# One twelve-bit product for gate and up in a pre-norm attention and quantised feed-forward kernel

## The chip, the cores and the metric

The kernel runs on one core of a Trainium2 chip. Its time is the device time of one execution in microseconds (us), the median over several runs. TensorE is written PE here, VectorE DVE, ScalarE ACT, GpSimd POOL; SP is the engine whose queue issues most transfers.

## The reference

One transformer layer on x of shape (2, 1024, 512): layer norm, attention with 32 heads of 16, residual; layer norm, a feed-forward part with quantised numbers, residual.

```python
x = x + attn(_layernorm(x), w_q, w_k, w_v, w_o)          # softmax(q k^T / 4) v, then w_o
x = x + ffn(_layernorm(x), w_gate, w_up, w_down, ...)

def int4_quant(x):                                        # integers -8..7 times a scale per token
    beta = jnp.mean(jnp.abs(x), axis=-1, keepdims=True)
    x_q = jnp.clip(jnp.round(x * SQRT7 / (beta + EPS)), -8, 7)
    return x_q * (beta * SQRT7) / SQRT7

def bitlinear(x, w, scale):                               # weights -1, 0, 1 times one mean
    w_mean = jnp.mean(jnp.abs(w))
    w_q = jnp.clip(jnp.round(w / (w_mean + EPS)), -1.0, 1.0)
    return jnp.einsum('...i,oi->...o', x, w_q * w_mean * scale)

xq = int4_quant(x)
gate = jnp.square(jax.nn.relu(bitlinear(xq, w_gate, s_gate)))   # w_gate, w_up: (1376, 512)
inter = int8_quant(bitlinear(xq, w_up, s_up) * gate)
return bitlinear(inter, w_down, s_down)                         # w_down: (512, 1376)
```

Inputs of gate and up are small integers and their weights are -1, 0 or 1, so their products are integers.

## The kernel before

**Attention.** The main loop goes through 32 steps, one for each batch, half of the queries (512), group of 128 features and half s of its heads (four heads at a time). A step has eight slots, one for each 128 keys. In each slot `scores` is called twice. It runs the row maxima of one step (`max_mm`, L475, reduced on DVE at L485) beside the exponentials of the step before (`exp_mm`, L515, ACT at L519). Both use fp32r matmuls on 32 rows of the array, and they share three pairs of PSUM banks in turn. Between the two calls `weigh_values` (L545) multiplies the exponentials of an earlier slot with V. After the last slot of two steps `normalise` divides by the sums, which go out to DRAM and back to be spread over rows; `normalise_last` does this on chip for the last pair, in four column blocks.

**Fillers.** Everything else is a generator that yields after each piece of work. The class `Fillers` keeps four lists (`proj`, `norm`, `ffn`, `back`) and steps them between the score calls, in the order of their due slots. A slot's second `fill.run` has a budget in nominal nanoseconds of PE, SHARE = 1300, or MORE = 1800 while a projection is due within 16 slots; pieces name their price in `yield ("pe", 900.0)`. A first `fill.run(100.0, short=True)` admits only short pieces. A piece that needs PSUM takes the spare bank (`ps_o`, one buffer) and gives it back for the next `run`; inside the loop no other bank is to be had. `_back` steps the `back` list and begins the first tasks of the `proj` and `norm` lists, so that their weights are fetched. `ensure` runs `fill.run(1e9)` until the named projections are done, just before a step's loads on SP (`load_k`, `load_q`, `load_v`). After the loop `fill.turn` steps every ready task once per round, and the score banks are spare too.

**Projections.** `project_qk` (L351) and `project_v` (L418) use plain fp32 matmuls. Q and K are split into a high and a low part: ACT copies PSUM to `full`, POOL makes `hi` and `lo`, SP stores both. `project_v` fetches its weights (L333) for each half of the tokens. The four `w` buffers are shared by all projections.

**Feed-forward.** `weight_sums` reads the three weight matrices once in pieces of 512 columns or less to get the means. `weight_quant` reads them again; POOL compares with the lower threshold (L677), DVE with the upper and subtracts (L679), and the results are kept in fp8. For each of 16 tiles of 128 tokens `output_proj` (L714) adds the residual and computes the statistics, `ffn_input` quantises and transposes, `ffn_product` (L801) multiplies, and `ffn_output` quantises `inter` (L841 to L853), transposes it and multiplies with `wd` (L880). The product takes the 1376 columns in chunks of 512, 512 and 352:

```python
for f, j in ((gate, 0), (gate, 1), (up, 0), (gate, 2), (up, 1), (up, 2)):
    yield from f(j)
```

`gate` is four matmuls, a Relu on ACT (L811) and a square (POOL L815, or ACT L813 for the last four tiles); `up` is four matmuls and one DVE multiply from PSUM (L823). The last four tiles can only start after the last step, so they run after the loop.

## Time and profile before

| | |
|---|---|
| median of 3 runs | 1307.87 us (1304.2 to 1317.62) |
| profiled execution: time, span | 1320.16 us, 1318.4 us |
| PE, DVE, ACT, POOL busy | 92%, 66%, 54%, 19% of the span |
| mean granted PE clock | 0.965 of full |
| PE idle, 66 to 264 us | 23.8 of 198 us |
| PE busy, 264 to 1188 us | 97 to 99% in the stretches of 132 or 66 us, except 264 to 396 and 924 to 1056 (96%) |
| last pso matmul ends | 1221.5 us |

Spans on PE are modelled: a matmul's record goes past the start of the next one, so the distance between starts tells more than a duration. In a line of the timeline the columns are start, duration, engine, line, operation, tiles and shapes; a bracket names the idle time before it and what ended it. In a line of groups, the number behind `x` is a count, then busy us and mean ns, then idle time of the engine and its releasers. A plain fp32 matmul is recorded as two.

### The profile page before, as it was taken

How to read it: one execution, taken by the hardware profiler on the slowest of the kernel's cores; microseconds unless marked ns; L12 is line 12 of the kernel's file. 1: busy time of each engine (PE TensorE's matmuls, PEld its weight loads, DVE VectorE, ACT ScalarE, POOL GpSimd, SP SyncE). 2: the span in 40 equal slices, each digit the busy share in tenths (PEclk: the TensorE clock that was granted, in tenths of full speed). 3: DMA queues.
4: the chain of work that ended last, by engine and by line, in shares of the span. 5: the costliest groups of instructions: out<-in, count | busy, mean ns of one | idle time of the engine just before them, and what ended most of it. 6: DMA issues, size and time to landing. Idle time of an engine off the chain costs nothing.

```text
span 1318.4 us, 22143 instructions
## 1 busy us (share of the span) xinstructions
PE 1209.3 (92%) x9082; PEld 541.6 (41%) x9082; DVE 866.5 (66%) x1203; ACT 712.1 (54%) x903; POOL 246.5 (19%) x279
## 2 busy tenths in 40 slices
PE   5768899999999999999999999999999999999566
PEld 2345444334445443444444444444433344443222
DVE  6521468778865667687776676877776867772634
ACT  1124655545655555665666556666665556666243
POOL 1034326455511100321101003110010111100000
PEclk9889999999999999999999999999999979999769
DMA  3056666555333431221213223211133110201000
GB/s 112 0 184 216 225 199 214 156 177 191 126 107 122 136 110 58 89 81 58 72 47 106 95 76 117 76 55 67 57 107 95 58 57 34 82 26 33 24 0 33
DMA packets 72334, 127.88 MB, mean 97 GB/s; under 512 B 9680, under 2 KB 30160, under 8 KB 72232
## 3 DMA queue, kind: packets, MB, share of 16 engines
q1 hardware_dynamic: 64360, 101.16, 23.8%
q0 software_dynamic: 7872, 25.30, 5.9%
q8 instruction: 71, 1.16, 0.4%
q14 instruction: 31, 0.25, 0.1%
HBM read 89.25 MB, written 37.19 MB: 96 GB/s over the span
## 4 chain that ended last, share of the span: by engine, by line
PE 74%; DVE 11%; ACT 5%; issue 4%; DMA 4%; POOL 2%; SPq 0%; ACTq 0%; DVEq 0%; POOLq 0%
PE pse L515 22%; PE pso L545 16%; PE psm L475 8%; PE psy L714 5%; PE psv L418 4%; DVE pm L485 4%; PE psq L351 3%; PE pu L801 3%; PE py L880 3%; PE psk L351 3%; DMA wv<-in_wvT 2%; PE pg L801 2%; ACT e L519 2%; PE psn L498 1%; PE psk L390 1%
## 5 line engine op out<-in xcount | busy, mean ns | idle before, releaser
L485 DVE TENSOR_REDUCE pm<-psm 128x2 f32<-128x1024 f32 x512 | 621.5, 1220 | 336.9 <-PE pse L515 236.8
L519 ACT ACTIVATE e<-pse 128x1024 f32<-128x1024 f32 x512 | 523.0, 1024 | 415.3 <-PE pse L515 315.4
L475 PE MATMUL psm<-kst,qst 32*128 32x512 f32 x2048 | 372.8, 448 | 13.4 <-ACT e L519 8.2
L515 PE MATMUL pse<-qst,kst 32*128 32x512 f32 x2048 | 371.7, 446 | 10.2 <-DVE pm L485 8.8
L515 PEld LDWEIGHTS pse<-qst,kst 32*128 32x128 f32 x2048 | 151.5, 185 | 325.0 <-issue 160.6
L545 PE MATMUL pso<-e,v 128*32 128x512 f32 x2048 | 277.5, 612 | 0.7 <-ACT po L554 0.4
L515 PE MATMUL pse<-mrow,onesr 2*128 2x512 f32 x1024 | 208.6, 406 | 0.0
L475 PEld LDWEIGHTS psm<-kst,qst 32*128 32x128 f32 x2048 | 152.5, 186 | 39.1 <-ACT e L519 27.9
L515 PEld LDWEIGHTS pse<-mrow,onesr 2*128 2x128 f32 x1024 | 95.3, 185 | 5.1 <-ACT mrow L502 0.2
L815 POOL TENSOR_TENSOR g<-g 128x512 f32<-128x512 f32 (+1 forms) x36 | 34.2, 951 | 315.6 <-ACT g L811 315.6
L418 PE MATMUL psv<-wv,xnT 128*128 128x128 f32 x512 | 70.7, 294 | 14.2 <-DMA wv<-in_wvT 12.0
L545 PEld LDWEIGHTS pso<-e,v 128*32 128x32 f32 x2048 | 40.7, 108 | 97.4 <-issue 94.5
L418 PEld LDWEIGHTS psv<-wv,xnT 128*128 128x128 f32 x512 | 64.0, 203 | 27.3 <-issue 19.7
L714 PE MATMUL psy<-wo,OT 128*128 128x512 f32 x128 | 66.7, 635 | 5.9 <-DVE OT L597 5.9
L351 PE MATMUL psq<-xnT,wq 128*128 128x512 f32 x120 | 60.9, 622 | 1.4 <-ACT full_k L359 1.4
L351 PE MATMUL psk<-xnT,wk 128*128 128x512 f32 x112 | 58.4, 640 | 1.5 <-ACT vst L430 1.5
L677 POOL TENSOR_SCALAR low<-raws,whalf 128x512 bf16<-128x512 f32 (+2 forms) x35 | 52.8, 1510 | 21.4 <-DMA raws<-in_wuT 8.5
L801 PEld LDWEIGHTS <-xqT 128*128 128x128 bf16 x384 | 33.1, 102 | 57.5 <-issue 38.0
L770 POOL TENSOR_SCALAR xn<-x,mv,a 128x512 f32<-128x512 f32 x12 | 24.9, 2073 | 166.8 <-DVE a L747 166.7
L801 PE MATMUL pg<-wg,xqT 128*128 128x512 fp8e4 (+1 forms) x192 | 49.9, 387 | 4.0 <-DVE inter L823 2.4
L801 PE MATMUL pu<-wu,xqT 128*128 128x512 fp8e4 (+1 forms) x192 | 47.6, 372 | 3.5 <-ACT g L811 2.5
L880 PE MATMUL py<-wd,iqT 128*128 128x512 fp8e4 (+1 forms) x176 | 45.1, 392 | 2.9 <-ACT g L811 1.7
(124 smaller groups left out, 841.6 us busy)
## 6 DMA issues: line engine op xcount, KB each, us to landing
v<-vD SPq DMA_DIRECT2D x32, 512.0 KB
kst<-kD SPq DMA_DIRECT2D x30, 512.0 KB
qst<-qD SPq DMA_DIRECT2D x60, 256.0 KB
vD<-vst POOLq DMA_DIRECT2D x32, 256.0 KB, 5.4
qD<-hi_q SPq DMA_DIRECT2D x30, 256.0 KB
qD<-lo_q SPq DMA_DIRECT2D x30, 256.0 KB
x<-in_x SPq DMA_DIRECT2D x16, 256.0 KB
wq<-in_wqT SPq DMA_DIRECT2D x16, 256.0 KB
```

The costliest lines, as they stand in the source:

```text
L351: nc.tensor.matmul(ps, w[:, c, :], xnT[b, h][:, c, :], start=(c == 0), stop=(c == KC - 1))
L418: nc.tensor.matmul(ps[:, i * P : (i + 1) * P], xnT[b, half][:, c, i * P : (i + 1) * P], w[:, c, :], start=(c == 0), stop=(c == KC - 1),)
L475: nc.tensor.matmul(ps[:, r % 2, :], qst[n][l][rows, t * P : (t + 1) * P], kst[n][rows, kh * QB : (kh + 1) * QB], start=(l == 0), stop=(l = ...
L485: nc.vector.tensor_reduce(pm[n][:, t, kh, 2 * j : 2 * j + 2], ps, AX.X, ALU.max, negate=True)
L515: nc.tensor.matmul(ps[:, r % 2, :], left, right, start=(l == 0), stop=(l == 2))
L519: nc.scalar.activation(e, ps, AF.Exp, scale=SCALE)
L545: nc.tensor.matmul(acc[n][32 * r : 32 * r + 32, :], vt[n][:, i, r, :], e[r // 2][:, r % 2, :], start=(i == 0), stop=(i == NT - 1),)
L677: nc.gpsimd.tensor_scalar(low, w, h[:rows, m, 1:2], None, ALU.is_lt)
L714: nc.tensor.matmul(ps, OT[b, h, g][:, i * P : (i + 1) * P], wo[g], start=(g == 0), stop=(g == NG - 1),)
L801: nc.tensor.matmul(ps, xT[:, c, :], w[:, c, n : n + size], start=(c == 0), stop=(c == KC - 1))
L815: nc.gpsimd.tensor_tensor(g2[j], g2[j], g2[j], ALU.mult)
L880: nc.tensor.matmul(py, iqT[:rows, c, :], wd[:rows, c, :], start=(c == 0), stop=(c == FC - 1))
```

## The change

Gate and up weights are kept in one fp32r matrix, `wgu = 3400 * up + gate`, each entry an integer of at most twelve bits. One product gives 3400 * U + G in PSUM. ACT divides by 3400 and rounds by adding and subtracting 1.5 * 2^23 (two passes), which gives U; DVE takes 3400 U away from PSUM, which leaves G. Relu, square and multiply then follow on POOL; for the last four tiles DVE does Relu and square in one step. The transposed inputs `xqT` become fp32r too.

```diff
+PACK = 3400.0
@@ ensure
-        while not set(names) <= self.done:
-            self.run(1e9)
+        tasks = [t for t in self.tasks["proj"] if t["name"] in names]
+        due = max((t["due"] for t in tasks), default=0)
+        while not set(names) <= self.done:
+            self._back()
+            task = 1
+            while task:
+                task = next(
+                    (t for t in self._candidates() if (t["due"] <= due and t["list"] == "proj" or t["kind"]) and self._ready(t)),
+                    None,
+                )
+                if task:
+                    self._step(task)
+            self.now += 1
@@ norm_inputs
-            nc.sync.dma_start(xs[t], x[b, t * P : (t + 1) * P, :])
+            (nc.scalar if fast and t % 2 else nc.sync).dma_start(xs[t], x[b, t * P : (t + 1) * P, :])
...
+            if fast and half == 0 and i % 2:
+                nc.vector.tensor_copy(dst, ps.rearrange("p (c t) -> p c t", c=KC))
+            else:
+                nc.scalar.copy(dst, ps.rearrange("p (c t) -> p c t", c=KC))
@@ project_qk
-        full = sb.tile([P, QB], F32, tag="full", name=f"full_{name}", bufs=1)
-        nc.scalar.copy(full, ps)
-        nc.gpsimd.tensor_copy(hi, full)
-        nc.gpsimd.tensor_tensor(lo, full, hi.bitcast(F32), ALU.subtract)
+        lo = sb.tile([P, QB], F32, tag="lo", name=f"lo_{name}", bufs=2)
+        nc.scalar.copy(lo, ps)
+        nc.gpsimd.tensor_copy(hi, lo)
+        nc.gpsimd.tensor_tensor(lo, lo, hi.bitcast(F32), ALU.subtract)
@@ project_v
-        w = proj_weights(wvT, g, f"wv_{b}_{g}_{half}")
-        yield ("gap", 4)
+        if half:
+            w = wt.pop((b, g, "v"))
+        else:
+            w = wt[b, g, "v"] = proj_weights(wvT, g, f"wv_{b}_{g}")
+            yield ("gap", 4)
@@ normalise_last (now a task of the back list)
+        OT[b, h, g] = ot
         for i in range(TQ):
+            if i == 2:
+                yield from done([f"out_{b}_{h}_0"])
...
+            fill.done.add(f"tokens_{i}")
+            yield ("gap", 1)
@@ load_raw, weight_sums: whole rows of 1376 columns (two of 512 for wd), two buffers
-        t = sb.tile([P, 512], F32, tag="raw", name=f"{name}{m}_{c}_{n}", bufs=4)
-        nc.gpsimd.dma_start(t[:rows, :cols], ap[c * P : c * P + rows, n : n + cols])
+        t = sb.tile([P, I], F32, tag="inter", name=f"{name}{m}_{c}", bufs=2)
...
+            nc.gpsimd.dma_start(part, ap[(c + i) * P : (c + i) * P + rows, :])
@@ weight_quant: order up, gate, down
+                low = below(m, c, part)
+                yield ("gap", 2)
...
+                    w = wgu[:, c, :]
+                    if m == 1:
+                        above(w, m, part, low, ALU.subtract)
+                    else:
+                        nc.vector.scalar_tensor_tensor(w, w.bitcast(F32), PACK, low, ALU.mult, ALU.subtract)
+                        yield ("gap", 1)
+                        above(w, m, part, w.bitcast(F32), ALU.add)
@@ output_proj
+                if last and g == NG - 1:
+                    yield from done([f"tokens_{i}"])
@@ ffn_input (DVE normalises only the first of the last four tiles, POOL the others)
+        first = last and i == 0
+        (nc.vector if first else nc.gpsimd).tensor_scalar(xn, xt, mean, a, ALU.subtract, ALU.mult)
@@ ffn_product
+            ps = spare(f"pgu_{k}_{n}")[:, :size]
             for c in range(KC):
                 nc.tensor.matmul(
-                    ps, xT[:, c, :], w[:, c, n : n + size], start=(c == 0), stop=(c == KC - 1)
+                    ps, xT[:, c, :], wgu[:, c, n : n + size], start=(c == 0), stop=(c == KC - 1)
                 )
...
+            nc.scalar.activation(up[j], ps, AF.Identity, bias=magic, scale=1.0 / PACK)
+            nc.scalar.activation(up[j], up[j], AF.Identity, bias=negmagic)
+            nc.vector.scalar_tensor_tensor(part, up[j], -PACK, ps, ALU.mult, ALU.add)
             yield ("give",)
             yield ("pe", 900.0)
+            if last:
+                nc.vector.scalar_tensor_tensor(part, part, 0.0, part, ALU.max, ALU.mult)
+            else:
+                nc.gpsimd.tensor_scalar(part, part, 0.0, None, ALU.max)
+                nc.gpsimd.tensor_tensor(part, part, part, ALU.mult)
+            nc.gpsimd.tensor_tensor(part, part, up.pop(j), ALU.mult)
@@ the order of the work
+                ready = ready + [name]
-    SHARE, MORE = 1300.0, 1800.0
+    SHARE, MORE = 1000.0, 1800.0
+        fill.WIDTH["proj"] = 4 if "first_1" in fill.done else 7
```

In `ffn_output` the last four tiles lose two pauses, and `cd` is computed after `inter` is scaled. V's second half now also waits for its first half.

## The prediction

> **What bounds the kernel now.** I read the page's busy shares and clock first, then busy time by stretch, the groups of instructions kept apart by shape, the chain of waits, and last the timeline of one ordinary slot, of the opening and of the end.
>
> ```profile
> PE 1209.3 (92%) x9082; PEld 541.6 (41%) x9082; DVE 866.5 (66%) x1203; ACT 712.1 (54%) x903; POOL 246.5 (19%) x279
> ...
> PEclk9889999999999999999999999999999979999769
> ```
>
> TensorE is the fullest engine. The share hides three stages, which the busy time by stretch shows (length, then PE, PEld, DVE, ACT, POOL busy, clock, DMA):
>
> ```profile
> 66.00:99.00 33.00, 21.00 (x125) 13.86 (x124) 7.07 (x6) 8.82 (x21) 10.99 (x20) 0.90 0.53 184
> 660.00:792.00 132.00, 130.24 (x1038) 58.55 (x1036) 93.11 (x122) 76.18 (x91) 8.48 (x9) 1.00 0.25 81
> 1253.00:1286.00 33.00, 22.77 (x87) 9.00 (x88) 12.42 (x26) 13.86 (x24) 0.00 (x0) 0.69 0.00 0
> ```
>
> From 264 to 1188 us PE is busy 96 to 99% of every stretch and DVE about 72%, so work taken off PE there shortens the run, unless a wait replaces it. Before 264 and after 1188 PE has holes, and chains of waits set the time.
>
> The middle, from the timeline of two slots (start, duration):
>
> ```profile
> 646.69 0.77 PE L801 MATMUL pu<-wu,xqT 128*128 128x352 fp8e4 x4
> 647.39 0.73 PE L515 MATMUL pse<-qst,kst 32*128 32x512 f32 x4
> ...
> 864.33 1.04 PE L801 MATMUL pu<-wu,xqT 128*128 128x512 fp8e4 x4
> 865.30 0.49 PE L515 MATMUL pse<-qst,kst 32*128 32x512 f32 x2
> ```
>
> A group of four product matmuls holds PE for 865.30 - 864.33 = 0.97 us at 512 columns and 647.39 - 646.69 = 0.70 us at 352. Without filler a slot is two score calls of 0.9 us and one pso of 1.0, some 2.85 us, against two 1.22 us reductions on DVE; so PE, not DVE, sets it.
>
> **Middle: product.** Removed: one of two product groups for each of 3 chunks, for 12 of the 16 tiles (the last four run after the loop). Per tile 2 x 0.97 + 0.70 = 2.64 us, times 12 = -31.7 us.
>
> The new product reads fp32r on 128 rows. No row shows that at 512 columns. From below: the fp32r score matmuls on 32 rows start in rounds 0.23 us apart (640.19, 640.42, 640.65 in that timeline), the pace of the fp8 group (0.97 / 4 = 0.24). From above: the four-fold fp32 of L351, 1.91 us for two matmuls, 0.95 each. psn (L498) is fp32r on 128 rows, at 128 columns: four in 0.66 us, each 0.29, so one per (0.66 - 0.29) / 3 = 0.12; four-fold would be 0.95 / 4 = 0.24. It is nearest in shape and not four-fold, so I take 0.24 us for 512 columns. An fp32 weight load lasts 185 to 203 ns against 102 for bf16; the later ones run under matmuls, the first of a chunk doesn't: 36 x 0.09 = +3.2 us.
>
> **Middle: unpacking.** These rows price it:
>
> ```profile
> L811 ACT ACTIVATE g<-pg 128x512 f32<-128x512 f32 x32 | 19.0, 595 | 12.6 <-PE pg L801 12.0 <-DVE d L845 0.6
> L813 ACT ACTIVATE g<-g 128x512 f32<-128x512 f32 x8 | 5.0, 629 | 0.3
> L887 DVE SCALAR_TENSOR_TENSOR y<-py,cd,x 128x512 f32<-128x512 f32 x16 | 11.9, 744 | 11.4 <-PE py L880 11.4
> L815 POOL TENSOR_TENSOR g<-g 128x512 f32<-128x512 f32 x24 | 24.9, 1040 | 224.2 <-ACT g L811 224.2
> ```
>
> A chunk needs ScalarE 0.60 + 0.63 us, then DVE 0.74, then GpSimd. Behind the second ScalarE pass queues the next slot's exponential (1.02 us), and the score call after pso waits for it to free its PSUM pair. Follow a slot from the end of a product, t = 0: the previous exponential ends at 0.2, the two passes at 1.43, the next exponential at 2.45; the second score call starts at 1.9 and wants the pair at 2.14. Stall about 0.35 us per chunk, 36 x 0.35 = +12.6 us. From below nothing is exposed (other filler lies between). From above, the wait seen behind other ScalarE work: 0.65 us of PE at 1179.59, after 1.43 + 0.45 us on ScalarE; with the DVE step behind it, 0.9 each, +32. DVE's queue too stands still until 1.43, then does 0.74 and two reductions, done at 4.7; the call needing the last pair comes near 6, so I price that at nothing; were that slack gone, each chunk would cost up to 0.74.
>
> GpSimd goes from 1.04 to about 1.6 + 1.04 + 1.04 = 3.7 us per chunk (1.6 from the L677 row). It is busy 8.48 of 132 us in the 660 stretch: nothing; without that cover the gm reduction, and the score reductions queued behind it on DVE, would wait 3.7 us.
>
> The budget of filler falls from 1300 to 1000 a slot. By the yields a tile's product falls from 5400 to 2700, the non-short work of a tile from 7900 + 3440 = 11340 to 8640: ratio 0.76 against 0.77. Costed at nothing; a tile left over would pay the tail's pace, 10.9 us.
>
> Middle: -31.7 + 3.2 + 12.6 = **-16** (bounds -32 to +4).
>
> **Weight preparation.** The GpSimd comparison keeps its total (L677, 52.8 us) but comes in pieces of 1606 x 1376 / 512 = 4.3 us; DVE has 12 steps of 2.0 us (L679, 745 ns, scaled) where there were 24 totalling 16.7. Queued behind them are reductions on DVE and the hi/lo splits on GpSimd; behind those the stores and loads on SP. Slots of 4.4 us (266 of them from 27 to 1203 us) leave DVE 2.0, so little shows: **+3** (0 to +8, 12 steps late by 0.7). Fewer, longer GpSimd fetches have one ahead in place of two or three; 5 to 7 us from issue to landing now, 8 us between uses then: nothing.
>
> **Opening.**
>
> ```profile
> 77.83 18.57 DMA wv<-in_wvT
> 96.53 6.65 PE psv L418 x32
> ...
> 135.51 14.31 DMA wv<-in_wvT
> 149.86 3.46 PE psv L418 x16
> ```
>
> These pieces of the chain are V weights arriving late: `ensure` runs any ready filler, so a V projection not yet due is put in PE's queue ahead of the scores and PE stops 8.7 us (and 3.3 at 149.86). The change fetches V weights once per pair and lets `ensure` run only what is due. The matmuls it skips run later, where PE is full: no gain. The 12.0 us of waiting go. Bounds: nothing, if another fetch is late (the held buffer blocks SP's queue: 4.7 us seen behind psv) and all of PE's holes from 66 to 264 us, 12.0 + 3.6 + 4.3 + 0 + 3.9 = 23.8. Splitting x over SP and ScalarE's queue (four issues took 1.81 us; ScalarE is idle until 12.99) is under 1 us, counted at nothing, like the split evacuation and the hi/lo split that now needs no `full` buffer. **-12** (-24 to 0).
>
> **End.** Now all four columns of the last normalisation precede the statistics: xq of the first tile is ready at 1252.0, the last column at 1231.1. After the change tiles 0 and 1 need two columns (1226.9), their last matmul 1.9, add 0.7, statistics 0.9, inverse root 2.5, absolute sums 1.9, factors 1.3, quantising 1.4: 1237.5, 14.4 us earlier. Columns 2 and 3 (4.2 us of DVE) and leftover output work compete: -10 (-14 to -4). The products then:
>
> ```profile
> 1254.78 1.87 PE L801 MATMUL pg<-wg,xqT 128*128 128x512 fp8e4 x4 [0.67 <-ACT xqT L782]
> ...
> 1257.33 1.86 PE L801 MATMUL pg<-wg,xqT 128*128 128x512 fp8e4 x4 [0.68 <-ACT g L811]
> ```
>
> One spare bank makes each chunk wait for its reader. The first tile takes 14.4 us (to 1269.16). With three chunks of 1.87 + 0.60 + 0.63 + 0.74 + 0.1 = 3.95, the last 2.9, and squaring and multiplying (1.4), 12.2. The other three take 10.9 each now; by the same sum 8.3 at full clock, 10.8 at half. I take 2.2 + 3 x 1 = -5 (-10 to 0). The 16 us after the last product stay. **-15** (-24 to -4).
>
> The granted clock from 1252 to 1270 was 0.50 with PE busy 12.1 of 18 us, and 1.00 from 1275. [...]
>
> **Sum.** -16 + 3 - 12 - 15 = -40. The profiled execution took 1320.2 us (span 1318.4, 1.8 around it), 0.9% above the median of 1307.87. 1320.2 - 40 = 1280; the same proportion off the median gives **1268 us**.
>
> **Rivals.** *Freed PE time comes back as idle time.* The chunk's stall is 0.8 us, the middle gains nothing, both ends gain: 1308 + 3 - 27 = 1284. For it: PE already waits at 1179.59; against: only 13.4 us of PE's idle time stands before psm. 0.13. *The ends give nothing*, the late fetch is replaced by another and the final chain by DVE's crowded queue: 1308 - 16 + 3 = 1295. For: SP and DVE keep their order; against: the waits are long and named. 0.07. *Slower: the spare bank.* In the loop filler has one bank, and it stays taken through both ScalarE passes and the DVE step, with an exponential ahead 3.1 us. If the next filler group, or short transposes 1.9 us after, meets it held, PE stops, scores behind it too. At 2 us a chunk: 36 x 2 + 3 - 32 = +43, with the ends -24: 1308 + 19 = 1327. It decides from (31.7 - 3.2 + 24) / 36 = 1.5 us a chunk. For: FIFO queues; against: 2.85 us of scores lie between. 0.09. *No single pass*: fp32r on 128 rows at L351's pace, 3.8 us a chunk for the 1.94 saved, on 48 chunks +90: 1308 + 90 - 24 = 1374. 0.03.
>
> **Numbers.** The forecast has 0.68 and its own range, 1236 to 1290; taking in the first two rivals gives 1236 to 1303. Over 1% is about what a measurement here tells from no change. Faster: 0.65 + 0.12 + 0.03 = 0.80; within 1%: 0.08; slower 0.12.
>
> **What would show it.** Right: one product group of about 1.0 us per chunk in the middle, 192 where L801 had 384 matmuls; PE's stalls before psm up by some 10 us; no stop of 8 us at psv; xq of the first of the last four tiles some 10 us sooner after the last pso. Wrong: a product matmul well over 0.24 us at full clock; PE idle in the middle by 30 us or more; filler still running long after the loop.

## The result, and the profile after

The changed kernel took **1354.88 us** (median of four runs, 1342.37 to 1363.15) against 1308.09 us before: ratio **1.0315 [1.0218, 1.0412]**, 3% slower where 3% faster was forecast. The run at 1363.15 us was in a slower state at a lower granted clock (0.930), and the ratio leaves it out, so it is smaller than that of the two medians. Its profiled execution took 1354.32 us, with a span of 1352.5.

The page of the changed kernel, busy time and granted clock:

```profile
PE 1208.1 (89%) x8890; PEld 554.0 (41%) x8890; DVE 884.2 (65%) x1203; ACT 734.5 (54%) x905; POOL 338.2 (25%) x318
...
PEclk9786999898999999999899999999999989898766
```

192 matmuls are gone (9082 to 8890), and PE's busy time fell by 1.2 us. The clock row has more eights than before. The busy time by stretch of the changed kernel, at the places shown of before (length, PE, PEld, DVE, ACT, POOL busy, clock, DMA share, GB/s):

```profile
66.00:99.00 33.00, 25.31 (x127) 14.37 (x126) 8.28 (x10) 9.78 (x16) 7.91 (x15) 0.90 0.47 165
660.00:792.00 132.00, 130.59 (x1019) 57.13 (x1011) 92.85 (x108) 80.13 (x91) 26.52 (x25) 1.00 0.27 82
1253.00:1286.00 33.00, 18.94 (x57) 11.16 (x58) 19.98 (x52) 11.35 (x18) 5.83 (x4) 0.71 0.00 1
```

PE is as full in the 660 stretch as it was (130.59 against 130.24), with half of the product gone: the freed time does not show as idle time there. The new product in the timeline of the changed kernel:

```profile
1096.17 1.20 PE L850 MATMUL pgu<-wgu,xqT 128*128 128x512 f32 x4
1097.30 0.50 PE L538 MATMUL pse<-qst,kst 32*128 32x512 f32 x2
...
1108.09 0.92 PE L850 MATMUL pgu<-wgu,xqT 128*128 128x352 f32 x4
1108.94 0.50 PE L538 MATMUL pse<-qst,kst 32*128 32x512 f32 x2
```

One group holds PE for 1.13 us at 512 columns and 0.85 at 352. The groups of instructions by shape, changed kernel (busy, mean ns | idle time before, and what ended it):

```profile
L498 PE MATMUL psm<-kst,qst 32*128 32x512 f32 x2048 | 380.5, 457 | 37.7 <-ACT e L542 32.7 <-DVE pm L508 3.6 <-ACT qst L415 0.7
...
L850 PEld LDWEIGHTS pgu<-wgu,xqT 128*128 128x128 f32 x192 | 37.0, 216 | 22.1 <-issue 13.2 <-ACT xqT L828 2.7 <-ACT iqT L914 2.0
...
L856 ACT ACTIVATE up<-up,negmagic 128x512 f32<-128x512 f32 x32 | 23.1, 722 | 1.1
L857 DVE SCALAR_TENSOR_TENSOR inter<-up,pgu 128x512 f32<-128x512 f32 x32 | 22.0, 686 | 54.0 <-ACT up L856 54.0
L855 ACT ACTIVATE up<-pgu,magic 128x512 f32<-128x512 f32 x32 | 21.9, 685 | 17.7 <-PE pgu L850 16.7
```

and the same score group of the kernel before:

```profile
L475 PE MATMUL psm<-kst,qst 32*128 32x512 f32 x2048 | 372.8, 448 | 13.4 <-ACT e L519 8.2 <-DVE pm L485 3.3 <-ACT vst L430 0.7
```

PE's idle time before psm, the matmuls of the row maxima, rose by 24 us. About half of that is not the product's, for in the version with two products again (apart, below) the same row has 25.5 us:

```profile
L499 PE MATMUL psm<-kst,qst 32*128 32x512 f32 x2048 | 375.3, 451 | 25.5 <-ACT e L543 20.1
```

VectorE stands at L857 for ScalarE's second pass. In the chain of waits of the changed kernel's opening the stops at V weights are gone; fetches of raw weights and a store of K's high part (kD) stand there instead:

```profile
68.15 7.43 PE psv L441 x64
77.71 5.13 DMA raw<-in_wgT
82.92 1.44 ACT junk L668 x2
...
93.27 10.29 DMA kD<-hi_k
```

By the profiles, the first exponential starts 5.4 us later than before (84.3 against 78.9), the last one 11.4 us later (1230.8 against 1219.4, where the profile of before has one stretch of 17 us at half rate; other profiles of that loop end it at 1208 to 1219), and the part behind it, "the end" from here on, takes 121.7 us instead of 99.0.

### The profile page after: what moved, and what is told of

It reads as the page before. It is cut to its first block, busy times and chain, and to the rows that moved or that the text cites. A ratio compares the mean times of both kernels' runs of the same rounds, so it can differ in the third digit from the quotient of the medians.

```text
span 1352.5 us, 21648 instructions
## 1 busy us (share of the span) xinstructions
PE 1208.1 (89%) x8890; PEld 554.0 (41%) x8890; DVE 884.2 (65%) x1203; ACT 734.5 (54%) x905; POOL 338.2 (25%) x318
## 3 DMA queue, kind: packets, MB, share of 16 engines
q8 instruction: 69, 1.13, 0.3%
q10 hardware_dynamic: 576, 1.05, 0.2%
## 4 chain that ended last, share of the span: by engine, by line
PE 68%; DVE 14%; ACT 8%; DMA 4%; issue 4%; POOL 2%; SPq 0%; POOLq 0%; ACTq 0%; DVEq 0%
PE pse L538 21%; PE pso L568 15%; PE psm L498 8%; PE psy L760 5%; DVE pm L508 5%; PE psv L441 4%; PE psk L372 3%; PE py L922 3%; ACT e L542 3%; PE psq L372 3%; PE pgu L850 2%; PE psk L410 1%; ACT up L856 1%; ACT iq L895 1%; PE psn L521 1%
## 5 line engine op out<-in xcount | busy, mean ns | idle before, releaser
L498 PE MATMUL psm<-kst,qst 32*128 32x512 f32 x2048 | 380.5, 457 | 37.7 <-ACT e L542 32.7
L568 PE MATMUL pso<-e,v 128*32 128x512 f32 x2048 | 283.1, 624 | 0.0
L863 POOL TENSOR_SCALAR inter<-inter 128x512 f32<-128x512 f32 (+1 forms) x36 | 49.2, 1367 | 188.0 <-DVE inter L857 185.7
L857 DVE SCALAR_TENSOR_TENSOR inter<-up,pgu 128x512 f32<-128x512 f32 (+1 forms) x48 | 30.3, 631 | 77.3 <-ACT up L856 77.2
L760 PE MATMUL psy<-wo,OT 128*128 128x512 f32 x128 | 73.1, 674 | 4.6 <-DVE OT L623 3.8
L865 POOL TENSOR_TENSOR inter<-inter,up 128x512 f32<-128x512 f32 (+1 forms) x48 | 56.4, 1176 | 63.8 <-DVE inter L861 56.5
L455 POOL DMA_DIRECT2D vD<-vst x32 | 18.4, 577 | 183.0 <-ACT vst L453 182.8
L850 PE MATMUL pgu<-wgu,xqT 128*128 128x512 f32 (+1 forms) x192 | 61.5, 447 | 2.9 <-DVE y L929 1.8
L815 POOL TENSOR_SCALAR xn<-x,mv,a 128x512 f32<-128x512 f32 x15 | 31.5, 2103 | 103.4 <-issue 56.5
L922 PE MATMUL py<-wd,iqT 128*128 128x512 fp8e4 (+1 forms) x176 | 50.0, 424 | 6.6 <-ACT iqT L914 4.4
```

Source lines behind the costliest of these rows:

```text
L498: nc.tensor.matmul(ps[:, r % 2, :], qst[n][l][rows, t * P : (t + 1) * P], kst[n][rows, kh * QB : (kh + 1) * QB], start=(l == 0), stop=(l = ...
L568: nc.tensor.matmul(acc[n][32 * r : 32 * r + 32, :], vt[n][:, i, r, :], e[r // 2][:, r % 2, :], start=(i == 0), stop=(i == NT - 1),)
L760: nc.tensor.matmul(ps, OT[b, h, g][:, i * P : (i + 1) * P], wo[g], start=(g == 0), stop=(g == NG - 1),)
L850: nc.tensor.matmul(ps, xT[:, c, :], wgu[:, c, n : n + size], start=(c == 0), stop=(c == KC - 1))
L863: nc.gpsimd.tensor_scalar(part, part, 0.0, None, ALU.max)
L865: nc.gpsimd.tensor_tensor(part, part, up.pop(j), ALU.mult)
```

## The experiments

"Loop" is the time from the first exponential's start to the last one's in the profiled execution. Loops, ends and slots come from one execution of each kernel, and the same code differs there: the five profiles of the loop of before (before and the four tail versions) end it between 1208 and 1219 us, and two with the end of tail_gaps take 94.9 and 100.1 us for it. A few us between two profiles say nothing by themselves; the ratios are of all runs. All were timed in five rounds against the kernel before, whose median was 1310 to 1312 us.

### The parts by themselves

**apart**: the changed kernel with two products in fp8 and the old budget.

```diff
-    wgu = const.tile([P, KC, I], F32R, name="wgu")
+    wg = const.tile([P, KC, I], FP8, name="wg")
+    wu = const.tile([P, KC, I], FP8, name="wu")
...
-    SHARE, MORE = 1000.0, 1800.0
+    SHARE, MORE = 1300.0, 1800.0
```

> The changed kernel with gate and up as two fp8 products again (and the slot budget of 1300 that belongs to them); opening, weight preparation and end stay as changed. Theory A (two places lose: the unpacking in the loop, and the order of the last four tiles): the loop gets back the 22 us that it lost between slot 88 and slot 256 and keeps the opening's gain, the end stays some 15 to 20 us longer than before: 1308 - 10 + 18 = 1316, ratio 1.00 to 1.01. Theory B (only the rebuilt end loses, the product is worth its 16 us): without the product it is slower than the changed kernel, 1365 to 1375, ratio 1.045. Theory C (only the unpacking loses, in the loop and after it): 1295 to 1300, ratio 0.99.

1326.61 us, ratio 1.0115 [1.0083, 1.0147]; last exponential 1209.9, end 114.6. Nearest to theory A, some 10 us above its time. So the packed product with its budget is worth about +2%, and something else about +1.1%.

**tail_only**: the kernel before with the rebuilt end (normalise_last by columns, output_proj in chained pairs, GpSimd normalising three tiles, no pauses in ffn_output).

```diff
+            if i == 2:
+                yield from done([f"out_{b}_{h}_0"])
...
+            fill.done.add(f"tokens_{i}")
+            yield ("gap", 1)
...
+                ready = ready + [name]
```

> The kernel before with the rebuilt end alone: normalisation of the last four column blocks as a task that waits after two, the second pair of output projections after the first, inputs of the last tiles on GpSimd but for one. Theory A (the order itself costs): columns 2 and 3 wait for the first pair's statistics, and the last two tiles come some 20 us late: 1323 to 1330, ratio 1.01 to 1.02. Theory C (the end loses because of the unpacking's latency and the half clock it causes): 1300 to 1310, or up to 10 us faster, ratio 0.99 to 1.00.

1325.16 us, ratio 1.0097 [1.0068, 1.0126]; end 115.0. The order of the end costs 1%, without any change in the product.

**opening_only**: the kernel before with the rebuilt opening.

```diff
-        w = proj_weights(wvT, g, f"wv_{b}_{g}_{half}")
-        yield ("gap", 4)
+        if half:
+            w = wt.pop((b, g, "v"))
+        else:
+            w = wt[b, g, "v"] = proj_weights(wvT, g, f"wv_{b}_{g}")
+            yield ("gap", 4)
```

> The kernel before with the rebuilt opening alone: V weights fetched once per pair, ensure limited to what is due, x over two queues, evacuation shared with VectorE, seven projections begun early. Theory (the waits on V weights go): slot 88 some 11 us sooner, and since the matmuls left out of ensure are only moved, the run 8 to 14 us shorter, 1294 to 1300, ratio 0.99. Rival (it is paid back in the full middle): the gain at slot 88 is there but the last exponential comes no sooner, 1305 to 1310, ratio 1.00.

1313.09 us, ratio 1.0005 [0.9982, 1.0029]. Against tail_only, whose opening is the old one, slot 8 is 9.0 us sooner, slot 32 10.3, slot 144 8.0, slot 192 3.3, and the last slot 0.5 (1211.5 against 1212.0): won, and gone by the end of the loop; by the whole time, the rival. Even the 9 us are not sure: tail_unchained (below), which also has the old opening, reaches slot 8 at 148.3 us, as early as opening_only (147.9), while before and tail_only need 159.6 and 156.9.

**share1300**: the changed kernel with the old budget.

```diff
-    SHARE, MORE = 1000.0, 1800.0
+    SHARE, MORE = 1300.0, 1800.0
```

> The changed kernel with the slot budget at 1300 instead of 1000. Theory A (pacing isn't the cause): within 8 us of the changed kernel, 1347 to 1363, ratio 1.03 to 1.04. Rival (thinner filler lets PE fall to half rate and lets work spill past the loop): 12 to 20 us faster, 1335 to 1343, ratio 1.02, and fewer half-rate stretches between 264 and 1188 us.

1371.98 us, ratio 1.0451 [1.0416, 1.0485]; last exponential 1253.8. Both were wrong: at the old budget the packed product is worse still.

### Where the matmul time of the product went

**double_product**: every packed group issued twice.

```diff
-            for c in range(KC):
+            for c in 2 * list(range(KC)):
```

> The changed kernel with the four matmuls of each packed product issued twice (eight into the same bank, the second four starting it anew; the result is the same). Each chunk costs TensorE another 1.13 us at 512 columns and 0.85 us at 352, 3.1 us a tile, 37 us over the twelve tiles inside the loop and 12 us over the four of the end. Theory A (TensorE's busy time is what the loop is made of, so that every microsecond of product is a microsecond of span): last exponential 33 to 40 us later than in the changed kernel (1230.8), the whole 1390 to 1405, ratio to the kernel before 1.06 to 1.07. Rival B (the time that the packed product freed on TensorE came back as waiting and as half rate, because the chain that takes the two products apart sets the pace): the added matmuls fall into that waiting, last exponential within 10 us of 1230.8, the whole 1350 to 1375.

1371.8 us, ratio 1.0453 [1.0412, 1.0493]; last exponential 1246.2. By the last exponential it lies between the two, by the whole time with rival B: 30 us of matmuls more in the loop cost 15 us.

**apart1000**: apart with the budget of 1000.

```diff
-    SHARE, MORE = 1300.0, 1800.0
+    SHARE, MORE = 1000.0, 1800.0
```

> The changed kernel with gate and up as two products, as before the change, now with the filler budget of 1000 of the changed kernel instead of 1300. Theory A (the budget matters only because the packed product charges 900 a chunk for 1.1 us of work and long unpacking; with two products it is neutral): within 4 us of the same kernel at 1300 (1326.6), ratio 1.008 to 1.014. Rival B (1000 is the better budget whatever the product): 8 us or more below it, ratio 1.005 or less.

1319.56 us, ratio 1.0057 [1.0036, 1.0078]: 7 us better, nearer to the rival. Of the 288 product matmuls of the loop's twelve tiles 28 now come after the loop. At equal budget the packed product is then 1.0315 / 1.0057, some 2.6% or 34 us, worse than two products.

**half_product**: apart1000 with half of each product's matmuls left out.

```diff
-            for c in range(KC):
+            for c in range(KC // 2):
```

> The changed kernel with two products and the budget of 1000 (1319.6 us, last exponential 1205.1), and with two of the four matmuls of each product group left out, so that gate and up are summed over half of their inputs only; every other instruction stays. That takes 28 us of matmuls out of the loop, about what the packed product takes out, with no unpacking. Theory A (TensorE's time is the span; the packed product lost by its unpacking alone): last exponential 22 to 30 us sooner, the whole 1284 to 1295, ratio 0.980 to 0.988. Rival B (thinner filler leaves TensorE waiting for the exponentials and reductions, and at half rate after, so that only about half of freed matmul time is had, as doubling the packed product cost only half of what it added): last exponential 8 to 16 us sooner, the whole 1298 to 1310, ratio 0.990 to 0.999.

1320.12 us, ratio 1.0068 [1.0046, 1.0091]; last exponential 1207.1. Neither: 25 us of matmuls fewer gave **nothing that can be told**. (The result is then that of half of the inputs.) The busy time over the loop as one stretch (length, PE, PEld, DVE, ACT, POOL, clock, DMA share, GB/s), apart1000 and then half_product:

```profile
84.60:1205.10 1120.50, 1081.84 (x8514) 479.56 (x8514) 765.10 (x941) 654.16 (x782) 213.23 (x201) 0.98 0.33 104
```

```profile
83.20:1207.10 1123.90, 1079.72 (x8384) 470.80 (x8384) 765.11 (x941) 653.31 (x781) 212.56 (x201) 0.97 0.32 104
```

The same stretches for the gate product's instructions alone (PE, then ACT), in the same order; the up product's rows have 30.52 and 18.34 us of PE:

```profile
84.60:1205.10 1120.50, 31.09 (x132) 18.18 (x33) 0.98 0.33 104
```

```profile
83.20:1207.10 1123.90, 18.31 (x66) 18.06 (x33) 0.97 0.32 104
```

Product rows fall from 61.6 to 36.7 us, PE's busy time only by 2.1: the records of the other matmuls, the same in number, cover 23 us more. "PE busy 97%" therefore did not say that PE set the pace. The distances from one matmul's start to the next, summed from the trace, say where the time went: the product's fall by 24.6 us, those of all others grow by 22.5, 9.8 of it behind the last two matmuls of an exponential call (pse<-mrow) and 6.7 behind psm. PE started its next work later there, and a modelled record can cover such waiting; the trace does not tell the two apart. The pages' chains, by engine, apart1000 and then half_product:

```profile
PE 77%; DVE 10%; ACT 5%; DMA 4%; issue 3%; POOL 1%; SPq 0%; ACTq 0%; POOLq 0%; DVEq 0%
```

```profile
PE 73%; DVE 12%; ACT 6%; DMA 4%; issue 4%; POOL 1%; SPq 0%; ACTq 0%; POOLq 0%; DVEq 0%
```

What PE loses of the chain, VectorE's reductions, ScalarE's exponentials and issue take over; the larger part stays with PE.

**half_before**: the same cut in the kernel before.

```diff
-            for c in range(KC):
+            for c in range(KC // 2):
```

> The kernel before with two of the four matmuls of each gate and up group left out, so that both products are summed over half of their inputs only. The loop's twelve tiles lose 144 matmuls, 31.5 us of rows at the product line, the end's four tiles some 6 to 10 us. Theory A (as in the version with two products and the budget of 1000, where the same cut gave nothing: the issue order ties each stretch of filler to an exponential and a reduction, and what TensorE does not spend on matmuls it spends waiting or at half rate): last exponential within 6 us of where it was (1208 to 1219 in undisturbed profiles), the whole 1300 to 1312, ratio 0.992 to 1.002. Rival B (the kernel before is TensorE's, as the forecast had it): last exponential 20 us or more sooner, the whole 1275 to 1290, ratio 0.973 to 0.984.

1300.53 us, ratio 0.9922 [0.9896, 0.9948]; last exponential 1202.1, end 91.4. By its whole time theory A, by its last exponential 6 us below A's range. (Here too the result is that of half of the inputs.) Against tail_unchained below (the same loop), 28.7 us of matmuls fewer shorten the loop by 8.6 us; the end gets 7.6 us shorter than before. So the kernel before would have given some 30% of a freed microsecond of product, with nothing to unpack; this is from one profile of each, and 8 of the 8.6 us can be the clock's, whose half-rate stretches cost 10.2 us here and 18.2 there. By start distances the other matmuls gain 9.9 us, 9.1 of it behind pse<-mrow again. In both cuts the pieces keep their price of 900 and the budget, so no other filler was let into the freed time; a cut with new prices was not tried.

The loops side by side, from the same view (PE's busy time, the product's rows, the difference, PE's idle time, granted clock):

| kernel | loop | PE busy | product | other PE | idle | clock |
|---|---|---|---|---|---|---|
| apart (two products, 1300) | 1126.0 | 1090.9 | 68.3 | 1022.7 | 35.1 | 0.98 |
| after (packed, 1000) | 1146.5 | 1090.6 | 40.4 | 1050.2 | 55.9 | 0.96 |
| double_product | 1161.4 | 1113.1 | 70.4 | 1042.7 | 48.3 | 0.97 |
| one_pass | 1131.7 | 1075.6 | 39.4 | 1036.3 | 56.1 | 0.97 |
| tail_unchained (loop of before) | 1133.7 | 1095.6 | 69.1 | 1026.5 | 38.1 | 0.98 |
| half_before | 1125.1 | 1077.0 | 40.4 | 1036.7 | 48.1 | 0.99 |

From apart to after: product -27.9, idle time +20.8, other matmuls +27.5, loop +20.5. The clock explains most of the third term: its half-rate stretches cost 42.7 us in the loop of after and 20.5 in that of apart, 22 us more.

### What unpacking costs

**one_pass**: a single ScalarE pass.

```diff
-            nc.scalar.activation(up[j], ps, AF.Identity, bias=magic, scale=1.0 / PACK)
-            nc.scalar.activation(up[j], up[j], AF.Identity, bias=negmagic)
-            nc.vector.scalar_tensor_tensor(part, up[j], -PACK, ps, ALU.mult, ALU.add)
+            nc.scalar.activation(up[j], ps, AF.Identity, bias=magic)
+            nc.vector.scalar_tensor_tensor(part, up[j], -PACK * MAGIC, ps, ALU.add, ALU.subtract)
```

> The changed kernel with a packing factor of 2048 and a single ScalarE pass: ScalarE adds 2048 times the rounding constant to the bank, VectorE takes the bank away from that (minus the gate's product is left; a minimum takes the place of the maximum), and GpSimd scales the rounded sum back to the up product in one more instruction. The second ScalarE pass (0.72 us a chunk, 0.55 at 352 columns) is gone, everything else stays. Theory A (the two ScalarE passes hold the bank and push back the exponentials behind them: the stalls of the scores rose from 13.4 to 37.7 us): last exponential 10 to 20 us sooner than the changed kernel's 1230.8, the whole 1330 to 1345, ratio to the kernel before 1.015 to 1.025. Rival B (the loss comes from TensorE itself, which falls to half rate when its queue has short pauses, whatever ScalarE does): within 5 us of the changed kernel, ratio 1.028 to 1.036.

(With a factor of 2048, gate products above 1024 run over into the up product, and by the reference the inputs give some up to about 1300: this kernel and one_pass_late then separate other values than the reference's, by the same instructions.) 1334.43 us, ratio 1.0171 [1.013, 1.0211]; last exponential 1214.9, 15.9 us sooner: theory A by size. But PE's idle time did not fall (56.1 against 55.9); of the loop's 15 us, 14 came from the other matmuls, at a higher clock.

**late_extract**: VectorE's extraction one turn later.

```diff
             nc.scalar.activation(up[j], up[j], AF.Identity, bias=negmagic)
+            yield ("gap", 1)
             nc.vector.scalar_tensor_tensor(part, up[j], -PACK, ps, ALU.mult, ALU.add)
```

> The changed kernel with VectorE's instruction that takes the gate's product out of the bank issued one turn of the filler later, so that a reduction of the scores is ahead of it in VectorE's queue; the bank is held that much longer. Theory A (VectorE stands at that instruction until ScalarE's two passes are done, 77 us in all, the reductions behind it come late, TensorE stalls, and each stall above about 1 us brings TensorE 3.4 to 10 us at half rate): that wait falls below 40 us, TensorE's idle time in the loop from 56 to 35 to 45 us, last exponential at 1208 to 1222 instead of 1230.8, the whole 1325 to 1345, ratio 1.010 to 1.025. Rival B (a bank held a turn longer delays the other fillers as much as VectorE wins): last exponential 1228 or later, ratio 1.028 or more.

1348.58 us, ratio 1.0294 [1.026, 1.0327]; last exponential 1230.2. From the waits, changed kernel and then this one (total, times, longest):

```profile
DVE inter L857 <- ACT up L856: 77.2, 40, 5.2
```

```profile
DVE inter L858 <- ACT up L856: 38.4, 10, 12.1
```

The wait fell by half, as theory A had it, and the loop did not move (PE's idle time in it is 55.0 us against 55.9). Theory A's gain is not there, and the numbers are rival B's: the bank, held a turn longer, may cost what VectorE wins. That neither costs anything would look the same, and this run does not tell the two apart.

**one_pass_late**: both, with the factor taken out by the input's copy.

```diff
+            nc.scalar.activation(up[j], ps, AF.Identity, bias=magic)
+            yield ("gap", 1)
+            nc.vector.scalar_tensor_tensor(part, up[j], -MAGIC, ps, ALU.add, ALU.subtract)
```

> The changed kernel with the packing factor 2048 taken out again by the copy of the transposed input, so that one ScalarE pass rounds the sum, VectorE's instruction subtracts, and GpSimd restores the up product in one more instruction; and with VectorE's instruction a turn later. Theory A (second ScalarE pass and VectorE's wait are two costs): last exponential at 1198 to 1212, the whole 1312 to 1332, ratio 1.000 to 1.015. Rival B (both take away the same wait): like the single pass alone, last exponential 1213 to 1218, ratio 1.015 to 1.019.

1336.76 us, ratio 1.021 [1.0185, 1.0234]; last exponential 1222.1. Neither; against one_pass the later turn again brings nothing.

**extra_pass**: apart1000 with one more ScalarE pass a chunk.

```diff
             else:
+                nc.scalar.activation(g2[j], g2[j], AF.Relu)
                 nc.gpsimd.tensor_tensor(g2[j], g2[j], g2[j], ALU.mult)
```

> The changed kernel with two products and the budget of 1000 (1319.6 us, last exponential 1205.1), with one more ScalarE pass over each gate chunk in the loop (a second Relu, which changes nothing), 0.6 us for each of 36 chunks, 22 us of ScalarE in all. Theory A (a ScalarE pass ahead of an exponential is what stalls TensorE, whatever the product): last exponential 8 to 16 us later, ratio 1.012 to 1.018. Rival B (two product groups give TensorE enough to do while ScalarE works; the pass hurts only beside the thin packed product): within 4 us, ratio 1.003 to 1.009.

1326.26 us, ratio 1.0101 [1.0066, 1.0135]; last exponential 1212.9, 7.8 us later. By the last exponential just short of theory A, by the ratio between the two: a ScalarE pass seems to cost even beside two full products, 7 us by the medians. The intervals of the two kernels overlap, so this is weaker than the rest.

How such a pass costs is seen in the changed kernel's timeline at one chunk (start, duration, instruction, idle time before):

```profile
884.44 0.72 ACT L856 ACTIVATE up<-up,negmagic 128x512 f32<-128x512 f32 x1
885.07 1.01 ACT L542 ACTIVATE e<-pse 128x1024 f32<-128x1024 f32 x1
...
886.12 0.50 PE L498 MATMUL psm<-kst,qst 32*128 32x512 f32 x2 [1.07 <-ACT e L542]
...
887.49 0.79 PE L538 MATMUL pse<-qst,kst 32*128 32x512 f32 x2
```

The second pass stands ahead of an exponential, PE waits 1.07 us for it, and 1.4 us later PE's rows last 0.79 us instead of 0.50. Sorting PE's stalls above 0.3 us from slot 88 on by what ran just ahead of their release: an exponential behind the second pass ended 8 stalls (6.9 us) in the changed kernel, none in apart, and one (0.4 us) in double_product, which has the same passes and twice the matmuls. In all, PE's stalls above 0.3 us there are 27.1 us in the changed kernel and 13.9 in apart, so these 8 are half of the difference.

### The end

**tail_nowait**: tail_only without the wait between columns.

```diff
-            if i == 2:
-                yield from done([f"out_{b}_{h}_0"])
```

> The kernel before with the rebuilt end, less the one wait by which the division of the last two columns of sums stands behind the output projection and statistics of the first pair; the second pair's projections still start after the first pair's. Theory A (that wait, 19 us between the second and the third column, is what makes the last two tiles late): the end after the last exponential shrinks from 115 to 100 us or less, the whole 1305 to 1313, ratio 0.995 to 1.002. Rival B (the chaining of the pairs' projections alone makes them late): still 110 to 115 us of end, ratio 1.006 to 1.010.

1328.15 us, ratio 1.0126 [1.009, 1.0162]; end 114.8. Not the wait.

**tail_unchained**: also without the chaining.

```diff
-                ready = ready + [name]
```

> The kernel before with the rebuilt end, less both the wait between the columns and the chaining of the second pair's output projections behind the first's; what stays is the division column by column with a release of each, the GpSimd normalisation of three tiles and the shorter way to the last quantisation. Theory A (the order in pairs is the whole loss of the rebuilt end): end after the last exponential 93 to 100 us, the whole 1300 to 1312, ratio 0.990 to 1.001. Rival B (the loss lies in the parts that stay, such as the normalisation on GpSimd, which then queues behind GpSimd's other work): still 110 us of end or more, ratio 1.007 or more.

1326.64 us, ratio 1.0123 [1.0085, 1.0161]; end 109.3. The end is 5 us shorter, the whole only 1.5 us, within the noise, so what the chaining costs is not shown; 10 us of the end remain, so most of the loss lies in parts that stay.

**tail_gaps**: also with the pauses of ffn_output as before the change.

```diff
         nc.vector.tensor_reduce(gm, v, AX.X, ALU.max, apply_absolute_value=True)
-        if not last:
-            yield ("gap", 1)
+        yield ("gap", 1)
```

> The kernel with the unchained rebuilt end, and with the three pauses of the issue order between the quantisation's steps (largest value, factors, scaling, rounding) put back as they are before the change. Theory A (without the pauses ScalarE's rounding of one tile is issued ahead of the next tile's passes over its product and waits in front of them for VectorE's 3.4 us chain, so that the tiles of the end follow each other at 14 to 18 us instead of 10 to 12): the end after the last exponential falls from 109.3 us to 93 to 101 us, the whole 1300 to 1312, ratio 0.992 to 1.001. Rival B (the normalisation of three tiles on GpSimd and the division's pauses make them late): still 107 us or more, ratio 1.007 to 1.013.

1309.68 us, ratio 0.9998 [0.9978, 1.0018]; end 94.9. The pauses were 14 us of the end and 1.25% of the whole: three yields that issue nothing (three, not the two that the section on the change counts), with VectorE's `cd`, an instruction of 0.2 us, back in its old place. ScalarE in the end, tail_unchained:

```profile
1269.15 0.63 ACT L816 ACTIVATE g<-g 128x512 f32<-128x512 f32 x1
1273.31 1.44 ACT L861 ACTIVATE iq<-inter,negmagic 128x1376 bf16<-128x1376 f32 x1 [3.53 <-DVE inter L855]
1274.66 0.58 ACT L814 ACTIVATE g<-pg 128x512 f32<-128x512 f32 x1
```

and tail_gaps:

```profile
1276.90 0.63 ACT L816 ACTIVATE g<-g 128x512 f32<-128x512 f32 x1
1277.44 0.58 ACT L814 ACTIVATE g<-pg 128x512 f32<-128x512 f32 x1
...
1284.39 1.43 ACT L856 ACTIVATE iq<-inter,negmagic 128x1376 bf16<-128x1376 f32 x1
```

Without pauses the rounding is issued ahead of the next tile's pass over its gate product and stands 3.53 us in front of it, waiting for VectorE's chain; with them it comes behind. ScalarE's waits at the rounding were, in tail_unchained and in tail_gaps:

```profile
ACT iq L861 <- DVE inter L855: 16.3, 4, 8.1
```

```profile
ACT iq L856 <- DVE inter L853: 2.7, 1, 2.7
```

Starts of the largest-value reduction (gm) of the last four tiles, after the last exponential:

| kernel | 1st | 2nd | 3rd | 4th | end |
|---|---|---|---|---|---|
| before | 51.1 | 63.0 | 72.7 | 83.2 | 99.0 |
| after | 45.8 | 62.8 | 90.3 | 106.0 | 121.7 |
| tail_only | 45.0 | 62.2 | 82.7 | 98.3 | 115.0 |
| tail_unchained | 43.2 | 61.6 | 79.1 | 93.4 | 109.3 |
| tail_gaps | 43.3 | 56.0 | 68.6 | 79.1 | 94.9 |

### Put together

**ap_gaps_un**: apart1000 with the mended end.

```diff
-            if i == 2:
-                yield from done([f"out_{b}_{h}_0"])
...
-                ready = ready + [name]
...
+        yield ("gap", 1)
```

> The changed kernel with two products and the budget of 1000, the pauses of the quantisation put back, the wait between the second and third column of sums and the chaining of the second pair of projections taken out: rebuilt opening and weight preparation, new budget, mended end. Theory A (the end's loss was the pauses and the chaining, and the budget of 1000 is better): end after the last exponential 95 to 103 us instead of 109.7, the whole 1302 to 1312, ratio 0.993 to 1.001. Rival B (the budget of 1000 only moves work of two tiles into the end, which then is as long as it was): 1314 or more, ratio 1.003 or more.

1322.2 us, ratio 1.0084 [1.0056, 1.0112]; end 109.3. The rival by its numbers: the smaller budget leaves 32 product matmuls of the twelve tiles for the end. But apart1000 left 28 and took 109.7 us for its end, so here the pauses and the unchaining, worth 20 us between tail_only and tail_gaps, gave nothing. That the leftover work hides them is argued, not tried.

**one_pass_gate_gaps**: the changed kernel with gate times 1024 plus up, one ScalarE pass, and the pauses put back.

```diff
-            nc.scalar.activation(up[j], ps, AF.Identity, bias=magic, scale=1.0 / PACK)
-            nc.scalar.activation(up[j], up[j], AF.Identity, bias=negmagic)
+            nc.scalar.activation(up[j], ps, AF.Identity, bias=magic)
...
+                nc.gpsimd.tensor_scalar(up[j], up[j], -MAGIC, 0.0, ALU.add, ALU.max)
```

> The changed kernel with the packing turned round: the gate's product times 1024 plus the up product, the factor taken out by the copy of the transposed input, so that one ScalarE pass rounds the sum to the gate's product, VectorE subtracts, and GpSimd removes the rounding constant and takes the maximum in one instruction; the pauses of the quantisation are put back as well. The result is the reference's. Theory A (one ScalarE pass less and the mended pauses add up): last exponential 1213 to 1220, end 103 to 110 us, the whole 1316 to 1328, ratio 1.004 to 1.013. Rival B (the pauses don't matter while the pairs are chained): end 115 us or more, ratio 1.015 to 1.020.

1325.38 us, ratio 1.0107 [1.0069, 1.0145]; last exponential 1214.4, end 103.2: theory A. The best packed version found takes back 2% of the 3.2% and is still behind the kernel before.

**opening_tail**: the kernel before with the rebuilt opening and the mended end.

```diff
+            w = wt[b, g, "v"] = proj_weights(wvT, g, f"wv_{b}_{g}")
...
+            fill.done.add(f"tokens_{i}")
+            yield ("gap", 1)
```

> The kernel before with the rebuilt opening and the rebuilt end, the end without the chaining of the projections and with the pauses of the quantisation kept; products, weight preparation and budget as before. Theory A (the opening's gain is paid back in the loop, the mended end gives 4 us): the whole 1303 to 1309, ratio 0.994 to 0.999. Rival B (nothing of either is left): 0.999 to 1.003.

1309.5 us, ratio 0.999 [0.9966, 1.0014]: no difference that can be told. No version tried is measurably faster than the kernel before and does all its work.

## Why the prediction was wrong

The 3.15% lie so, by ratios: the end's order +0.97 (tail_only), opening and reading the weights in whole rows +0.18, within the noise (apart less tail_only), the budget -0.58 (apart1000 less apart), the packed product, with VectorE's packing of the weights, +2.58 (after less apart1000).

**What bounds the kernel** is the step that failed first. From "96 to 99% of every stretch" I read that work taken off PE shortens the run, unless a wait replaces it, and priced the wait at 12.6 of 31.7 us. half_before and half_product, which add no work at all, measured what is left: at most 30% of the freed time, and nothing. The slot sum behind it (2.85 us of scores against 2.44 us of reductions) left out what else VectorE and ScalarE do in the same slot; that this is the reason is not shown. The sign of being wrong that the prediction named came: from 264 to 1188 us PE is idle for 36.3 us, against 22.0 before.

**Middle: product, -31.7 + 3.2.** As matmul time nearly right: one group of 1.13 and 0.85 us (I had 0.24 a matmul and 0.09 for the first weight load, 1.05 together), product rows down by 27.9 us in the loop. fp32r on 128 rows takes 0.28 us a matmul, with weight loads of 216 ns, against 0.95 for the plain fp32 of L351. One of the starts that I quoted for the pace from below, 640.19, is a weight load's; the score matmuls start at 640.09, 640.42 and 640.65. As a term of the span it was worth between nothing and 30%.

**Middle: unpacking, +12.6.** The mechanism I followed (passes, then the exponential behind them, then PE) is the one seen at 884 us. The passes took 0.69 and 0.72 us, not 0.60 and 0.63, and I priced a stall at its own length, without the half rate behind it: the loop has 20.8 us more idle time than that of apart and loses 22 us more to the clock. Not all of this is the unpacking's, since the cuts, with nothing to unpack, raised the idle time too, by 5.5 and 10 us. What is left for it, an estimate: the loop grew by 20.5 us against apart although the product fell by 27.9, worth 0 to 8 us, so 20 to 29 us; against apart1000 26.0 and 21.2, so 26 to 32 us. One pass alone is 15 us of the loop (one_pass). My upper bound of +32 rested on 0.65 us at 1179.59, which is the wait of a weight load; PE itself waited 0.21 us there.

**VectorE's queue at nothing** and **GpSimd at nothing** are not settled. Halving VectorE's wait changed nothing, with a bank held longer (late_extract); one_pass gave GpSimd another instruction a chunk and was faster, but for another reason, and VectorE's reduction to the largest value (gm) waited 5.8 us for GpSimd inside the loop of the changed kernel.

**The budget at nothing** was wrong with either product: 1000 instead of 1300 is worth 7 us with two products and 18 us with the packed one (share1300 less after).

**Weight preparation, +3**: +2 together with a neutral opening, within the noise; not separated further.

**Opening, -12.** The waits went, as said, and the early slots came 8 to 10 us sooner than in tail_only, though not than in tail_unchained. That they stay so was wrong: by the last slot the gain was 0.5 us, and the whole gained nothing (opening_only). I had argued that the skipped matmuls run later "where PE is full: no gain" and still kept the 12 us.

**End, -15.** The first tile came sooner, but by 5 us at its gm (51.1 to 45.8), not the 10 forecast at its xq. I followed the first tile only; the fourth came 23 us later. The edit that cost most, the pauses taken out of ffn_output, is not in my sum at all (+14). The chaining, at most +5, I had left to "leftover output work compete". What remains of the rebuilt end without both gains nothing that can be told (tail_gaps, opening_tail).

**The rivals.** "Freed PE time comes back as idle time" was right in kind at a chance of 0.13, but priced at 0 for the middle and kept the ends' gain. The slower rival named the spare bank; two runs held a bank a turn longer and neither clearly gained nor lost (late_extract, one_pass_late), which speaks against it as the main cause but, with VectorE relieved in the same edit, does not rule it out.

**What stays open.** In half_product some 7 of the 23 us by which other matmuls grew are the clock's (its half-rate stretches cost 34.1 us in that loop and 27.3 in that of apart1000); what PE waited for in the rest is not settled. Nor is why the budget matters more for the packed product, why one_pass left the idle time as it was, or why the mended end gave nothing beside the smaller budget. The packed product's loss is measured, but only the second pass's part of it, 1.4 of 2.6%, by a run of its own.

## What to carry to other kernels

A busy share near 100% is no proof that an engine sets the pace (here 97% of the loop of apart1000, and 25 us of matmuls fewer gave nothing that can be told): take half of the work in question out of it, without adding anything, and see what the span gives, before paying for that time elsewhere. A pause in an issue order that issues nothing can be what lets another tile's work go ahead (here ScalarE waited 2.7 us at the rounding with the pauses and 16.3 without), so its removal is an edit to be priced like an added wait. Follow the last tile of a final chain, not the first.

## What the hardware showed

A stall of PE can be followed by a loss beyond its length, in the rows below 2.59 us and then 10.2 us at half rate. In the changed kernel's loop the trace's clock records show 12 stretches at half rate, of 3.4 to 20.5 us, 85.3 us in all; 4 begin during a stall of 0.9 us or more, 8 within some 3 us after the end of one. That each stall above about 1 us brings one, as theory A of late_extract had it, is not shown: behind slot 88 there are 16 stalls of 0.9 us or more and 7 stretches, of 3.4 to 10.2 us. In apart's loop the half rate comes to 41.0 us. One such stretch, in the changed kernel's timeline, in its busy time by stretch (all engines), and in that of the pso rows, the products of the exponentials with V, alone (PE, PEld, ACT):

```profile
1078.87 0.40 PE L498 MATMUL psm<-kst,qst 32*128 32x512 f32 x2
1081.85 0.79 PE L538 MATMUL pse<-qst,kst 32*128 32x512 f32 x2 [2.59 <-DVE pm L508]
```

```profile
1082.00:1092.00 10.00, 10.00 (x58) 4.05 (x62) 6.54 (x13) 3.77 (x6) 1.72 (x1) 0.50 0.01 2
1092.00:1102.00 10.00, 7.76 (x67) 3.27 (x64) 7.30 (x11) 6.42 (x7) 2.26 (x2) 1.00 0.02 2
```

```profile
1082.00:1092.00 10.00, 3.87 (x16) 0.40 (x16) 0.00 (x0) 0.50 0.01 2
1092.00:1102.00 10.00, 2.13 (x16) 0.31 (x16) 0.00 (x0) 1.00 0.02 2
```

PE idles for 2.59 us and then runs 10 us at half rate, with no pause in them: sixteen pso matmuls take 3.87 us instead of 2.13. All seven stretches behind slot 88 came with pauses of 0.9 to 2.6 us. That the stalls bring it about is read from this order in the records, not tried by itself.
